# A graph-attention layer: scores by seven block products onto seeded PSUM banks, masks of a whole batch at once, one listed order for all engines of the loop

## The chip, the cores and the metric

The kernel runs on one core of one Trainium2 chip. Five engines of that core work beside each other, each through its own instructions in their written order: PE (TensorE, matrix products into PSUM), DVE (VectorE), ACT (ScalarE), POOL (GpSimd) and SP (SyncE, which here only issues DMAs). They wait for each other through semaphores. The metric is device microseconds of one execution, and lower is better; the time of a kernel is the median of several executions.

## The reference, cut to what matters

`x` is 16 batches x 512 nodes x 512 features. There are 16 heads of 32 features, 20 neighbours (the first 20 nodes of a batch), 11 edge labels and two directions.

```python
self_feat = concat(x, where(x.sum(-1) == 0, 0, q)) @ W_self.T + b_self
output = self_feat
for d in range(2):
    A = (adj if d == 0 else adj.swapaxes(1, 2))[:, :, :20]      # 512 x 20 x 11 labels
    cond, vb = A.sum(-1), A @ w_bias + b_bias
    kv = self_feat[:, :20]
    qh, kh = heads(self_feat @ Wq[d].T + bq[d]), heads(kv @ Wk[d].T + bk[d])
    aff = einsum('bnhd,bmhd->bnhm', qh, kh) / sqrt(32)
    w = softmax(where(cond > 0, aff, -9e15) + vb, axis=-1)      # over the 20 neighbours
    output += per_head_output(einsum('bnhm,bmf->bnhf', w, kv), Wout[d], bout[d])
return x + relu(output)
```

## The kernel before

All is float32, and features lie on the 128 partitions in four chunks (`C`). A set-up stage loads the weights, makes the neighbours' features and keys, and folds `Wq` into the keys: a batch then has a matrix `g` (512 features x 608 columns; 608 is 16 heads x 2 directions x 19, since the scores of neighbour 0 are subtracted from the others). The `g` of batches 2 to 15 are written to DRAM (`g_d`) from staging tiles `st` and read back by the loop. The set-up ends with a run of PE bursts (`keys`, line 696) between which other products are put.

The loop goes over 16 batches, and in a batch over four tiles `nt` of 128 nodes. For each tile:

- PE: `scores` (line 356). Two halves `g` of 64 nodes, four feature chunks `k` and two halves `a` of the heads make 16 matrix products of a 128x64 stationary block with 304 moving columns; a float32 product is two passes, so the trace has 32 instructions for a tile. The two halves `a` go to different halves of the PE's columns and run side by side.
- POOL: `full_add` (line 346) adds key bias and mask of the tile into `full`.
- DVE: `weigh` adds scores and `full` (369), takes the largest of each 20 (373) and subtracts it (377). ACT: `expo` (382). DVE: `normal` sums (415) and inverts (416); POOL multiplies (417). DVE: `turn` transposes the weights into `wt` (406, 408).

Once in a batch: `product` (line 283) makes the features of the *next* batch by seven products of half-size blocks (n = 1 to 7, 16 instructions each) in place of eight, whose terms `partial` (290) and `joined` (300) put together on DVE and whose operands `x_sum` (248) makes on POOL. `mask_mul` (318), `mask_count` (323, 324), `mask_sum` (329) and `mask_spread` (337) make the masks in two halves of 256 nodes. `attend` (435) multiplies the weights `wt` of the batch before with its values `vd` into four PSUM banks; `finish` adds `self_feat` to them on DVE (459), applies the bias and the relu on ACT (463), and `residual` adds `x` on POOL (468).

The order is the order in which the loop's code issues the steps; a planner isn't involved. The last batch has a path of its own: its last tile is worked in two halves, and `self_feat`, bias and `x` are put into the output banks by PE (`put_self`, 803) ahead of `attend`, so that little is left behind the last product.

Of the kernel before, what the change touches and what calls it, by code (L numbers as in the profile page):

```python
# [18 lines left out]
def gat_kernel(  # L19
# [66 lines left out]
    g0 = const.tile([P, C, WD], F32, name="g0")  # L86
# [9 lines left out]
    xs, xns, rss, adjs, nzs, sfs, cqs, gs, vds = {}, {}, {}, {}, {}, {}, {}, {}, {}  # L96
    adds, fulls, wts, outs, held, sf_ps, conds, prods = {}, {}, {}, [], [None] * 3, {}, {}, {}
    sums, parts, us, done = {}, {}, {}, {}


    def behind(one, other):

        if other is not None:
            info = mybir.DependencyInfo(mybir.DependencyClass.Sync, mybir.DependencyReason.DATA)
            tc.add_manual_dep(one.ins, other.ins.name, info, reason="loads in turn")
# [87 lines left out]


    def self_feat(b, f, h, parts=((0, range(C)), (1, range(C)))):


        lo, hi = max(NG, h * N // 2), (h + 1) * N // 2
        for i, ks in parts:
            if (i, ks[0]) == (0, 0):  # L200
                if (f, h) == (0, 0):
                    new_self(b)
                held[0] = bank(f"ps_sf{b}_{f}{h}", 3 if (f, h) == (1, 1) else None)
            for k in ks:
                for a in range(HA):
                    nc.tensor.matmul(  # L206
                        held[0][bass.ts(a, RA), i * N // 2 : i * N // 2 + hi - lo],
                        ws_v[:, k, bass.ds((2 * f + i) * P + a * RA, RA)], xs[b][:, k, lo:hi],
# [5 lines left out]
    def self_copy(b, f, h):  # L214

        lo, hi = max(NG, h * N // 2), (h + 1) * N // 2
        ps = sf_ps.pop((b, f, h))
# [32 lines left out]
    def product(b, n):  # L250
# [11 lines left out]
        if n == 1:  # L262
            parts[b, "a"] = [bank(f"ps_a{b}_{i}", i) for i in range(2)]
        if n == 2:
            parts[b, "d"] = bank(f"ps_d{b}", 2)
        if n == 5:
            parts[b, "c"] = bank(f"ps_c{b}", 3)
# [811 lines left out]
```

## Time and profile before

| what | value |
|---|---|
| median of 3 runs | 587.99 us (587.1 to 588.12) |
| profiled execution | 589.11 us, of which 587.3 us are the span that the profile covers |
| mean granted PE clock | 0.994 |
| busy share of the span | PE 98%, DVE 85%, POOL 65%, ACT 50% |

The profile gives, for each engine, busy time and groups of instructions by line; a timeline gives start and length of each run of equal instructions, and what an engine that stood idle waited for. The times of a PE run include the tail in which its last columns drain, so the distance from one start to the next says what a run costs. In the rows, the part ahead of `<-` is what is written, the part behind it what is read; `x32` is a count.

### The profile page before, as it was taken

The numbers are of one execution on the slowest core, as the hardware profiler recorded it, in microseconds if no ns is written. First come the engines' busy times: TensorE is split into PE (matmuls) and PEld (weight loads), VectorE is DVE, ScalarE is ACT, GpSimd is POOL, SyncE is SP. The second block draws the span as 40 slices with busy tenths as digits, with TensorE's granted clock in tenths as the row PEclk, the third lists the DMA queues.
The fourth block names the chain that finished last, engine by engine and source line by source line (L and its number), as shares of the span: only waits on it lengthen the run. The fifth ranks groups of instructions, "written<-read, shape, count | busy, mean of one in ns | idle before, by whom it ended". The sixth has DMA issues, their size and how long they took to land.

```text
span 587.3 us, 15688 instructions
## 1 busy us (share of the span) xinstructions
PE 578.5 (98%) x6188; PEld 353.2 (60%) x6188; DVE 497.3 (85%) x850; ACT 296.4 (50%) x778; POOL 382.0 (65%) x351
## 2 busy tenths in 40 slices
PE   8999999999999999999999999999999999999995
PEld 5444547886666665656565656565666656666654
DVE  0495565889999999999998989898989899999996
ACT  1234442546464646555564646464747474645441
POOL 2315663658677776858585868685858585867774
PEclk9999999999999999999999999999999999999997
DMA  8999999855858484868586767667665757582513
GB/s 298 382 404 312 349 371 322 243 146 159 232 153 242 150 249 158 246 153 237 150 247 164 215 172 227 173 212 197 177 207 183 222 167 228 159 242 68 169 37 127
DMA packets 93434, 125.56 MB, mean 214 GB/s; under 512 B 11217, under 2 KB 65521, under 8 KB 91313
## 3 DMA queue, kind: packets, MB, share of 16 engines
q1 hardware_dynamic: 92112, 122.67, 68.0%
q0 software_dynamic: 672, 1.36, 1.1%
q8 instruction: 49, 0.80, 0.5%
q10 hardware_dynamic: 576, 0.53, 0.3%
q14 instruction: 25, 0.20, 0.1%
HBM read 85.71 MB, written 39.19 MB: 213 GB/s over the span
## 4 chain that ended last, share of the span: by engine, by line
PE 94%; DVE 3%; DMA 1%; issue 0%; ACT 0%; SPq 0%; POOL 0%; DVEq 0%; POOLq 0%; ACTq 0%
PE ps_s L356 44%; PE ps_a L283 17%; PE ps_c L283 8%; PE ps_o L435 6%; PE ps_d L283 4%; PE ps_v L671 3%; PE ps_k L607 3%; PE ps_sf L206 2%; DMA ws_q<-in_wsT 1%; PE ps_kv L557 1%; DVE o L459 0%; PE ps_nz L190 0%; DVE ps_s L373 0%; DVE full L369 0%; DVE sm L415 0%
## 5 line engine op out<-in xcount | busy, mean ns | idle before, releaser
L356 PE MATMUL ps_s<-g,sf 128*64 128x304 f32 x2048 | 273.6, 420 | 0.5 <-ACT st L711 0.5
L356 PEld LDWEIGHTS ps_s<-g,sf 128*64 128x64 f32 x2048 | 152.1, 137 | 107.5 <-issue 6.2
L417 POOL TENSOR_TENSOR s<-s,sm 128x640 f32<-128x640 f32 x63 | 80.2, 1273 | 130.4 <-DVE sm L416 127.9
L382 ACT ACTIVATE s<-s 128x640 f32<-128x640 f32 x63 | 46.5, 737 | 163.6 <-DVE s L377 163.6
L318 ACT ACTIVATE prod<-adj,wb_sb 128x80 f32<-128x80 int32 x330 | 111.6, 427 | 0.0
L346 POOL TENSOR_TENSOR full<-cq,both 128x640 f32<-128x640 f32 x64 | 99.5, 1555 | 2.7 <-ACT both L337 1.5
L369 DVE TENSOR_TENSOR full<-ps_s,full 128x608 f32<-128x608 f32 x63 | 49.8, 791 | 31.4 <-PE ps_s L356 26.1
L468 POOL TENSOR_TENSOR o<-o,x 128x512 f32<-128x512 f32 x60 | 75.5, 1279 | 0.0
L337 ACT COPY both<-add 64x80 f32<-64x80 f32 x128 | 32.8, 256 | 52.0 <-DVE add L329 50.6
L283 PE MATMUL ps_a<-t,ws_s 128*64 128x246 f32 x480 | 55.1, 371 | 0.0
L373 DVE TENSOR_REDUCE ps_s<-full 128x32 f32<-128x640 f32 x63 | 52.2, 828 | 2.2
L377 DVE TENSOR_TENSOR s<-full,ps_s 128x640 f32<-128x640 f32 x63 | 51.5, 818 | 1.1
L415 DVE TENSOR_REDUCE sm<-s 128x32 f32<-128x640 f32 x63 | 50.8, 806 | 1.6 <-ACT s L382 0.9
L406 DVE STREAM_TRANSPOSE wt<-s 128x512 f32<-128x512 f32 (+1 forms) x65 | 45.3, 696 | 0.1
L283 PEld LDWEIGHTS ps_a<-t,ws_s 128*64 128x64 f32 x480 | 35.5, 137 | 15.9
L435 PE MATMUL ps_o<-wt,vd 32*32 32x256 f32 (+4 forms) x1360 | 42.8, 382 | 1.5 <-DVE wt L408 1.5
L329 DVE TENSOR_REDUCE add<-prod 128x80 f32<-128x960 f32 x32 | 36.8, 1150 | 5.9 <-ACT prod L318 3.9
L463 ACT ACTIVATE o<-o,bo 128x512 f32<-128x512 f32 x60 | 38.2, 710 | 1.2 <-POOL biased L911 1.2
L248 POOL TENSOR_TENSOR t<-x 128x492 f32<-128x492 f32 x30 | 34.4, 1148 | 4.9 <-DVE full L369 4.9
L435 PEld LDWEIGHTS ps_o<-wt,vd 32*32 32x32 f32 (+1 forms) x1360 | 26.2, 122 | 17.6 <-issue 12.2
L459 DVE TENSOR_TENSOR o<-ps_o,sf 128x512 f32<-128x512 f32 x60 | 36.7, 668 | 0.0
L290 DVE SCALAR_TENSOR_TENSOR u<-nz,qw,ps_a 128x246 f32<-128x246 f32 x90 | 36.6, 448 | 0.0
(238 smaller groups left out, 766.6 us busy)
## 6 DMA issues: line engine op xcount, KB each, us to landing
g_d<-st SPq DMA_DIRECT2D x16, 1064.0 KB, 5.7
g<-g_d SPq DMA_DIRECT2D x28, 608.0 KB, 4.9
out_T<-o SPq DMA_DIRECT2D x60, 256.0 KB, 4.5
xn<-in_xn SPq DMA_DIRECT2D x28, 512.0 KB, 3.6
x<-in_xT SPq DMA_DIRECT2D x28, 512.0 KB, 4.4
adj<-in_adj SPq DMA_DIRECT2D x32, 440.0 KB, 4.4
vd<-bd_d SPq DMA_DIRECT2D x64, 64.0 KB, 3.9
nz<-nz_d SPq DMA_DIRECT2D x14, 256.0 KB, 3.4
```

The source lines that it names most:

```text
L283: nc.tensor.matmul(to, lhs, x[:, k], start=start, stop=stop, skip_group_check=n != 2)
L318: nc.scalar.activation(p[:, :, l], a[:, :, l], AF.Identity, scale=wb_sb[:, l : l + 1])
L346: nc.gpsimd.tensor_add(f, cqs[b].unsqueeze(1).to_broadcast(shape), adds[b, nt // 2][:, nt % 2].unsqueeze(2).to_broadcast(shape),)
L356: nc.tensor.matmul(bank[bass.ts(a, RA), :WA], sfs[b][:, k, bass.ds(nt * P + g * RA, RA)], keys[:, k, a], start=(k == 0), stop=(k == C - 1),)
L369: nc.vector.tensor_add(f[:, :, :, 1:], ps[:, :, :WA].rearrange("p g (h m) -> p g h m", m=ND), f[:, :, :, 1:])
L373: nc.vector.tensor_reduce(mx, f, AX.X, ALU.max)
L377: nc.vector.tensor_sub(s, f, mx.unsqueeze(3).to_broadcast(full))
L382: done["exp"] = nc.scalar.activation(sw, sw, AF.Exp)
L415: nc.vector.tensor_reduce(sm, s, AX.X, ALU.add)
L417: done["normal"] = nc.gpsimd.tensor_mul(s, s, sm.unsqueeze(3).to_broadcast(full))
L435: nc.tensor.matmul(banks[q][to, bass.ts(c, w)].rearrange("p (t g n) -> p t g n", g=HA, n=32), lhs, rhs, start=start and first and c == 0, ...
L468: nc.gpsimd.tensor_add(o[:, c], o[:, c], xs[b][:, c])
```

## The change

**Scores.** The nodes of a batch are put in another order (two halves of 256 that each begin with ten of the neighbours), and nodes, features and heads are split so that the score matrix of a batch is a 2x2 by 2x2 block product. It is made by seven block products (`score_product`, P1 to P7) in place of eight: 16 products of 128x64 with 152 moving columns each (4 tiles of 64 nodes, `j`, x 2 feature chunks x 2 halves `a`). Their operands need sums: of blocks of `self_feat` (`self_sum`, S1 to S4) and of blocks of the keys (`key_sum`, T2, T1, T4), all on POOL; one difference of the key weights is taken in the set-up (`weight_differences`).

**Seeds.** The PSUM banks are held for the whole loop: `ps_a`, `ps_w`, `ps_e` (two banks each), `ps_u`, `ps_v` (one each). Products are never started afresh in the first three: ACT writes the starting value (key bias into `ps_a`, masks into `ps_w`, a difference of key biases into `ps_e`, `self_feat` with its bias into the output banks, which are `ps_w` and `ps_e` again), and PE adds. ACT and DVE copy intermediate sums out of `ps_a` (`u1`, `u2p`, `u3p`). The softmax works on four units of 2x64 x 4 tiles (c11, c22, c21, c12), each [128 x 640] as before; mask and bias no longer pass through `full`, and `full_add` and `finish` are gone. The features' seven products go through `ps_u` and `ps_v` with such seeds too.

**Masks** of a batch are made at once: 11 multiplications of 160 rows on ACT in place of 22 of 80, one count and one sum on DVE, and four copies in place of eight.

**Order.** One list gives every step of every engine for a batch, with the distance in batches (`P1:0` this batch, `f1:-1` the next, `OUT:1` the one before, `reluW:2` the one before that). The loop runs it from period -3 to 19 and leaves out what is not there. The last batch has no path of its own any more.

```diff
-    def scores(b, nt, g, bank, ks=range(C)):
-        keys = gs[b].rearrange("p c (a w) -> p c a w", a=HA)
-        for k in ks:
-            for a in range(HA):
-                nc.tensor.matmul(
-                    bank[bass.ts(a, RA), :WA], sfs[b][:, k, bass.ds(nt * P + g * RA, RA)], keys[:, k, a],
-                    start=(k == 0), stop=(k == C - 1),
-                )
+    def score_product(b, n):
+        rows, keys, to = {
+            1: (lambda: self_block(b, 0, 0), lambda: key_block(b, 0), ps_a),
+            2: (lambda: self_block(b, 0, 1), lambda: key_block(b, 1), ps_w),
+            3: (lambda: sums[b, "s", 4], lambda: key_block(b, 2), ps_e),
+            4: (lambda: self_block(b, 1, 1), lambda: sums[b, "t", 4], ps_a),
+            5: (lambda: sums[b, "s", 1], lambda: sums[b, "t", 1], ps_e),
+            6: (lambda: sums[b, "s", 2], lambda: sums[b, "t", 2], ps_a),
+            7: (lambda: sums[b, "s", 3], lambda: key_block(b, 3), ps_a),
+        }[n]
...
+        for k in range(2):
+            for j in range(C):
+                for a in range(HA):
+                    nc.tensor.matmul(
+                        to[bass.ts(a, RA), j, :, 1:], rows[:, k, bass.ts(j, RA)],
+                        keys[:, k, a].rearrange("p (x m) -> p x m", m=ND),
+                        start=False, stop=k == 1, skip_group_check=True,
+                    )
+    def seed_scores(b):
+        nc.scalar.copy(grid(ps_a), over_groups(cqs[b][:, 0]))
+    def first_part(b):
+        us[b, "1"] = score_part(b, 1)
+        nc.scalar.copy(us[b, "1"], grid(ps_a))
+    def masked_part(b, n):
+        us[b, str(n)] = score_part(b, n)
+        nc.vector.tensor_add(by_head(us[b, str(n)]), by_head(grid(ps_a)), mask_of(b, n - 2))
+    def unit(b, i, l):
+        t = soft_w[b, i, l] = soft.tile([P, C, FW], F32, tag=f"s{i}{l}", name=f"s{b}_{i}{l}", bufs=1)
+        if (i, l) == (1, 0):
+            nc.vector.tensor_add(by_head(t), by_head(grid(ps_a)), mask_of(b, 1))
+        else:
+            n, of = {(0, 0): ("1", ps_w), (0, 1): ("2", ps_e), (1, 1): ("3", ps_e)}[i, l]
+            nc.vector.tensor_add(t, grid(of), us.pop((b, n)))
+    def mask_mul(b):
+        for l in range(L):
+            nc.scalar.activation(label_sums(b)[:, :, l], labels(b)[:, :, l], AF.Copy, scale=wb_sb[:, l : l + 1])
+    def seed_out(b, a):
+        for c in range(HA):
+            n = a * HA + c
+            nc.scalar.activation(out_banks(a, c), turned(sfs[b][:, n]), AF.Identity, bias=bo[:, n : n + 1])
+    order = """
+        S3:0 sr21:1 P1:0 Lv:1 reluW:2 S2:0 tr11:1 Lcq:-1 reluE:2 sr12:1 f1:-1 nm21:1 Lt3:-1 u1:0 cnt:-1 seedE:0
...
+        soE:1 sb21:0 ex12:0 nm22:0 OUT:1 ex21:0 j12:-1 cfin:-1 seedA:-1 S1:-1 tr22:0 Lnz:-2
+        clear_blocks(zero)
+        for period in range(-3, B + 4):
+            for name, back in order:
+                b = period - back
+                if 0 <= b < B and (name, b) not in made:
+                    steps[name](b)
+            if period == 0:
+                blocks()
```

What this does to the order is shown at three places, where `x16` counts products (two passes each) and a name's last number tells buffers apart.

PE, one batch in the middle of the loop, before (`ps_s`: scores of a tile; `ps_a`, `ps_c`, `ps_d`: features of the next batch), starting behind `attend`:

```order
L356 MATMUL ps_s_2_2154<-g_1931,sf_1951 64x304 x16
L283 MATMUL ps_a_0_2244<-x_2065,ws_v 64x246 x4
L283 MATMUL ps_a_1_2245<-x_2065,ws_v 64x246 x4
L283 MATMUL ps_d_2254<-x_2065,ws_v 64x246 x8
L283 MATMUL ps_a_0_2244<-t_2_2148,ws_s 64x246 x4
L283 MATMUL ps_a_1_2245<-t_2_2148,ws_s 64x246 x4
L356 MATMUL ps_s_3_2281<-g_1931,sf_1951 64x304 x16
```

The same engine after the change, from behind `attend` on (`ps_a`, `ps_w`, `ps_e`: P1, P6, P2, P5, P7, P4, P3; `ps_u`, `ps_v`: features; two more feature products and `attend` follow):

```order
L413 MATMUL ps_a<-g_1101,sf_2758 64x8x19 x16
L277 MATMUL ps_u<-x_2827,ws_v 64x246 x8
L413 MATMUL ps_a<-k_2_2813,s_2_2958 64x8x19 x16
L413 MATMUL ps_w<-g_1101,sf_2758 64x8x19 x16
L413 MATMUL ps_e<-k_1_2829,s_1_2922 64x8x19 x16
L413 MATMUL ps_a<-g_1101,s_3_2929 64x8x19 x16
L277 MATMUL ps_u<-t_2_3068,ws_s 64x246 x8
L413 MATMUL ps_a<-k_4_2834,sf_2758 64x8x19 x16
L277 MATMUL ps_v<-x_2827,ws_v 64x246 x8
L413 MATMUL ps_e<-g_1101,s_4_3115 64x8x19 x16
L277 MATMUL ps_u<-t_3_3140,ws_s 64x246 x8
L277 MATMUL ps_v<-t_1_3040,ws_s 64x246 x8
```

Four runs of 304-column products have become seven of 152-column ones, and `ps_a` is filled four times in a batch, each time after somebody has read it.

POOL where set-up and loop meet, before (`full`: mask and bias of a tile, `t`: operands of the feature products, `s`: softmax weights):

```order
L720 COPY g_81<-st_1031 128x152
L346 TENSOR_TENSOR full_1_1112<-cq_749,both_0_748 128x640
L248 TENSOR_TENSOR t_1_1114<-x_171 128x492
L417 TENSOR_TENSOR s_0_1107<-s_0_1107,sm_0_1129 128x640
L248 TENSOR_TENSOR t_2_1176<-x_171,t_1_1114 128x492
```

And after (`k`: sums of key blocks T2, T1, T4; `s`: sums of feature blocks S1, S3, S2):

```order
L785 COPY g_79<-st_1033 128x152
L430 TENSOR_TENSOR cqd_1112<-cq_751 128x160
L386 TENSOR_TENSOR k_2_1121<-g_79 128x608
L386 TENSOR_TENSOR k_1_1123<-g_79,k_2_1121 128x608
L386 TENSOR_TENSOR k_4_1125<-g_79,k_2_1121 128x608
L396 TENSOR_TENSOR s_1_1128<-sf_718 128x512
L396 TENSOR_TENSOR s_3_1130<-sf_718 128x512
L396 TENSOR_TENSOR s_2_1148<-s_1_1128,sf_718 128x512
L251 TENSOR_TENSOR t_1_1216<-x_172 128x492
```

Six sums now stand on POOL between the last key block and the second score product, which reads the first and the last of them.

DVE in the second half of a batch, after (`s_10`, `s_01`, `s_11`: softmax units 21, 12, 22; `sf<-ps_v`: features joined):

```order
L447 TENSOR_TENSOR s_10_2054<-ps_a,both_1681 128x640
L307 TENSOR_TENSOR sf_2006<-ps_v,f_1_1877 128x2x246
L460 TENSOR_REDUCE ps_a<-s_10_2054 128x32
L450 TENSOR_TENSOR s_01_2079<-ps_e,u_2_1914 128x640
L460 TENSOR_REDUCE ps_a<-s_11_2008 128x32
L460 TENSOR_REDUCE ps_e<-s_01_2079 128x32
L464 TENSOR_TENSOR s_11_2008<-s_11_2008,ps_a 128x640
L307 TENSOR_TENSOR sf_2006<-ps_v,f_3_2093 128x2x246
L464 TENSOR_TENSOR s_01_2079<-s_01_2079,ps_e 128x640
```

Before, add, maximum and difference of one tile stood behind each other there:

```order
L369 TENSOR_TENSOR full_1_2107<-ps_s_1_2111,full_1_2107 128x32x19
L373 TENSOR_REDUCE ps_s_1_2111<-full_1_2107 128x32
L377 TENSOR_TENSOR s_1_2142<-full_1_2107,ps_s_1_2111 128x640
L406 STREAM_TRANSPOSE wt_2145<-s_0_2100 128x512
L408 STREAM_TRANSPOSE wt_2145<-s_0_2100 128x128
```

Now three units are taken in turn, and the difference of unit 12 (the last row above) releases the ACT seed of `ps_e` that `attend` adds to.

More of the change, by code (lines that the diff above doesn't have):

```diff
@@ L94, in gat_kernel @@
     nz_d = dram.tile([B, N], F32, name="nz_d")
[L96 to L105, printed above, removed]
@@ L261, in product @@
         x = x()
[L262 to L267, printed above, removed]
+        to = ps_v if n in (2, 3, 5) else ps_u
         for i in range(2):
@@ new lines, in feature_seed, with feature_join, label_sums @@
+    def feature_seed(b, f):
+        for i in range(2):
+            nc.scalar.activation(
+                ps_v[:, bass.ts(i, HN)], nzs[b][:, half(f)], AF.Copy, scale=qw[:, 2 * f + i, b : b + 1]
+            )
+    def feature_join(b, f, l, n):
+        nc.vector.tensor_add(sfs[b][:, 2 * f : 2 * f + 2, half(l)], side(ps_v), us.pop((b, n)))
+    def label_sums(b):
+        if b not in prods:
+            prods[b] = msk.tile([P, C * S, L + 1], F32, tag="prod", name=f"prod{b}", bufs=1)
+        return prods[b]
@@ L335, in mask_spread, with mask_sum @@
+    def mask_sum(b, rows=slice(0, C * S)):
+        if rows.start == 0:
+            sums[b, "mask"] = msk.tile([P, C * S], F32, tag="add", name=f"add{b}", bufs=1)
+        nc.vector.tensor_reduce(sums[b, "mask"][:, rows], prods[b][:, rows], AX.X, ALU.add)
+    def mask_spread(b, units=(0, 1), halves=range(HA)):
+        at = slice(units[0], units[-1] + 1)
+        if b not in both:
+            both[b] = msk.tile([P, 2, C, S], F32, tag="both", name=f"both{b}")
         for a in halves:
             for g in range(HA):
-                nc.scalar.copy(
-                    adds[b, h][bass.ts(a, RA), :, g], add[bass.ts(g, RA)].rearrange("p (t m) -> p t m", t=2)
-                )
@@ L426, in attend @@
-    def attend(b, banks, tiles=slice(0, NT), start=True, stop=True):
-        n = tiles.stop - tiles.start
-        w = n * HA * 32
-        heads = wts[b][:, tiles, : W * 4 // 5].rearrange("p t (g j n) -> p t g j n", g=HA, n=32)
-        ends = wts[b][:, tiles, W * 4 // 5 :].rearrange("p t (g j n) -> p t g j n", g=HA, n=32)
-        def mm(q, c, to, lhs, rhs, first):
+                to = both[b].rearrange("p i (y x) m -> p i y x m", x=HA)[bass.ts(a, RA), at, :, g]
+                of = sums[b, "mask"].rearrange("p (i y m) -> p i y m", i=2, m=S)[bass.ts(g, RA), at]
@@ L437, in mm @@
-                start=start and first and c == 0, stop=stop and not first, skip_group_check=True,
+                (ps_w, ps_e)[a][to, g, bass.ts(c, NH)].rearrange("p (i j n) -> p i j n", i=2, n=32), lhs, rhs,
+                start=False, stop=True, skip_group_check=True,
             )
@@ L685, in gat_kernel, with weight_differences @@
             HB = B // 2
+            def weight_differences(hg):
+                low, high = (wq_sb[:, :, hg, bass.ts(j, HF)] for j in range(2))
+                nc.gpsimd.tensor_sub(low, high, low)
             def keys(runs):
@@ new lines, in gat_kernel @@
+    made = {
[3 rows of a table added]
+    }
+    made = {(name, b) for b, names in made.items() for name in names.split()}
+    order = """
+        S3:0 sr21:1 P1:0 Lv:1 reluW:2 S2:0 tr11:1 Lcq:-1 reluE:2 sr12:1 f1:-1 nm21:1 Lt3:-1 u1:0 cnt:-1 seedE:0
+        Lk21:-1 res3:2 seedD:0 P6:0 cu1:-1 Lk22:-1 nm12:1 lab:-1 tr21:1 St3:2 P2:0 xs1:-1 u2p:0 Lk11:-1 tr12:1
+        cqd:-1 res1:2 P5:0 c11:0 xs2:-1 St1:2 mx11:0 sb11:0 res0:2 P7:0 ex11:0 xs4:-1 Ladj1:-2 sd:-1 f6:-1 u3p:0
+        msc:-1 rs34:-2 St0:2 sr11:0 S4:0 P4:0 Ladj2:-2 nself:-1 c22:0 rs12:-2 xs3:-1 u2s:-1 nm11:0 soW:1 lsum:-1
+        f2:-1 Lxn1:-3 fl:-2 res2:2 P3:0 Snz:-2 Lxn2:-3 c21:0 spread:-1 T2:-1 j11:-1 mx21:0 sc:-1 f7:-1 Lx2:-2
+        T1:-1 c12:0 mx22:0 T4:-1 f5:-1 mx12:0 cu3:-1 St2:2 sb22:0 Lx1:-2 f4:-1 ex22:0 j22:-1 sb12:0 sr22:0 f3:-1
+        soE:1 sb21:0 ex12:0 nm22:0 OUT:1 ex21:0 j12:-1 cfin:-1 seedA:-1 S1:-1 tr22:0 Lnz:-2
```

705 lines of the change are left out of this document (276 added, 429 removed), and 3 rows, old and new, of the table made.

## The prediction, on record before the run

> **What bounds the kernel now.** I read the page's totals and its chain first:
>
> ```profile
> span 587.3 us, 15688 instructions
> PE 578.5 (98%) x6188; PEld 353.2 (60%) x6188; DVE 497.3 (85%) x850; ACT 296.4 (50%) x778; POOL 382.0 (65%) x351
> PE 94%; DVE 3%; DMA 1%; issue 0%; ACT 0%; SPq 0%; POOL 0%; DVEq 0%; POOLq 0%; ACTq 0%
> ```
>
> PE is the bound: it is never idle, and the chain that ended last is PE for 94%. Next the timeline of PE over one batch, and busy times of all engines in that stretch:
>
> ```profile
> 305.79 4.26 PE L356 MATMUL ps_s<-g,sf 128*64 128x304 f32 x32
> 309.88 1.83 PE L283 MATMUL ps_c<-x,ws_s 128*64 128x246 f32 x16
> 311.54 4.26 PE L356 MATMUL ps_s<-g,sf 128*64 128x304 f32 x32
> 315.73 2.57 PE L435 MATMUL ps_o<-wt,vd 32*128 32x256 f32 x80
> 318.23 4.32 PE L356 MATMUL ps_s<-g,sf 128*64 128x304 f32 x32
> 322.38 1.83 PE L283 MATMUL ps_a<-x,ws_v 128*64 128x246 f32 x16
> ...
> 336.45 1.45 PE L356 MATMUL ps_s<-g,sf 128*64 128x304 f32 x10
> ```
> ```profile
> 305.79:336.45 30.66, 30.66 (x323) 18.65 (x321) 28.25 (x48) 17.30 (x48) 21.88 (x19) 1.00 0.71 198
> ```
>
> By the starts: scores of a tile 4.09 us, a feature product 1.66, attend 2.50; 4 x 4.09 + 7 x 1.66 + 2.50 = 30.48, and the batch lasts 30.66. So 0.18 is stall and the rest is columns. The second row gives PE, PEld (weight loads), DVE, ACT, POOL: 30.66, 18.65, 28.25, 17.30, 21.88.
>
> **Scores.** 4.09 us for 32 instructions of 304 columns, two side by side, is 0.256 per pair, 0.84 ns a column. Seven products of 16 pairs and 152 columns are 112 x 0.128 = 14.32 us, if nothing but columns counts; now 16.36. The nearest rows for short runs are these (a set-up burst, whose four row groups run side by side; then weight loads; then the narrowest products):
>
> ```profile
> 70.73 0.29 PE L696 MATMUL ps_g(2, 2, 1, 0, 2)0_846<-khD,wq_sb 32*128 32x152 f32 x2
> 70.86 0.29 PE L696 MATMUL ps_g(2, 2, 1, 0, 2)0_846<-khD,wq_sb 32*128 32x152 f32 x2
> L356 PEld LDWEIGHTS ps_s<-g,sf 128*64 128x64 f32 x2048 | 152.1, 137 | 107.5 <-issue 6.2 <-ACT st L711 0.7
> L803 PE MATMUL ps_o<-biased,ident 128*128 128x64 f32 x16 | 2.0, 279 | 0.0
> ```
>
> 152 columns follow each other after 0.13 us there, though each needs a new load of 128 columns. A 64-column load takes 137 ns, but two run side by side (152.1 / 2048 = 74 ns each). The narrowest, with 128-column loads, still cost 125 ns each (2.0 / 16). Bounds for a pair: 0.128 (columns alone) and 0.149 (two loads of 74 ns in turn). I take 0.128, by the 152-column rows. Features and attend keep their sizes: PE per batch 14.32 + 11.62 + 2.50 = 28.44; with a stall as now, 28.6.
>
> [...]
>
> **The other engines must fit into 28.6.**
>
> ```profile
> L369 DVE TENSOR_TENSOR full<-ps_s,full 128x608 f32<-128x608 f32 x63 | 49.8, 791 | 31.4 <-PE ps_s L356 26.1 <-issue 3.1 <-POOL t L248 2.2
> L373 DVE TENSOR_REDUCE ps_s<-full 128x32 f32<-128x640 f32 x63 | 52.2, 828 | 2.2
> L415 DVE TENSOR_REDUCE sm<-s 128x32 f32<-128x640 f32 x63 | 50.8, 806 | 1.6 <-ACT s L382 0.9
> L459 DVE TENSOR_TENSOR o<-ps_o,sf 128x512 f32<-128x512 f32 x60 | 36.7, 668 | 0.0
> L329 DVE TENSOR_REDUCE add<-prod 128x80 f32<-128x960 f32 x32 | 36.8, 1150 | 5.9 <-ACT prod L318 3.9 <-POOL prod L324 2.0
> L290 DVE SCALAR_TENSOR_TENSOR u<-nz,qw,ps_a 128x246 f32<-128x246 f32 x90 | 36.6, 448 | 0.0
> L300 DVE TENSOR_TENSOR sf<-ps_c,u 128x492 f32<-128x492 f32 x30 | 19.3, 645 | 0.0
> L318 ACT ACTIVATE prod<-adj,wb_sb 128x80 f32<-128x80 int32 x330 | 111.6, 427 | 0.0
> L382 ACT ACTIVATE s<-s 128x640 f32<-128x640 f32 x63 | 46.5, 737 | 163.6 <-DVE s L377 163.6
> L463 ACT ACTIVATE o<-o,bo 128x512 f32<-128x512 f32 x60 | 38.2, 710 | 1.2 <-POOL biased L911 1.2
> L417 POOL TENSOR_TENSOR s<-s,sm 128x640 f32<-128x640 f32 x63 | 80.2, 1273 | 130.4 <-DVE sm L416 127.9
> L346 POOL TENSOR_TENSOR full<-cq,both 128x640 f32<-128x640 f32 x64 | 99.5, 1555 | 2.7 <-ACT both L337 1.5
> L468 POOL TENSOR_TENSOR o<-o,x 128x512 f32<-128x512 f32 x60 | 75.5, 1279 | 0.0
> ```
>
> DVE loses `finish` (4 x 0.67) and gains two 640-wide adds (`u2p`, `u3p`, 2 x 0.82, scaled from 608); one count and one sum of twice the length save about 0.3: 28.25 - 2.67 + 1.64 - 0.3 = 26.9. It stays 1.7 under PE.
>
> ACT gains `u1` and three seeds (4 x 0.74), four output seeds (4 x 0.71), two feature copies (2 x 0.6, between 320 and 512 wide) and four half-width seeds (4 x 0.45): 8.8. The 22 label multiplications become 11: now 111.6 / 15 = 7.4 us a batch, then between 11 x 0.43 = 4.7 (width free) and again 7.4 (width is all). 17.3 + 8.8 - 2.7 to 0 is 23.4 to 26.1.
>
> POOL loses four `full_add` (6.2) and gains four S (1.28 each), three T (608 wide, between 1.28 and 1.56, taken 1.42) and one short difference (0.5): 21.9 - 6.2 + 5.1 + 4.3 + 0.5 = 25.6.
>
> So all three fit by sums. SP's queue carries the same bytes (198 GB/s in the row above) in another order: value loads and `Lcq` first, then the keys between the stores, then adjacency, `xn` and `x`. The adjacency now has one buffer: its load waits for the multiplications and the count of the batch before, and has most of a period to land. `Lx2` waits for the last residual add of two batches ago, and behind it stand the other half, a store and the flags; the first reader comes some 12 us later. I cost this at nothing; the cover is that distance, and if it goes, xs1 and f1 are late. The set-up's two weight differences (POOL, 1.28 each) lie beside the key products and cost nothing either.
>
> Waits in the steady loop. DVE instructions that don't wait for each other overlap a little:
>
> ```profile
> 569.62 0.82 DVE L377 TENSOR_TENSOR s<-full,ps_s 128x640 f32<-128x640 f32 x1
> 570.36 0.70 DVE L406 STREAM_TRANSPOSE wt<-s 128x512 f32<-128x512 f32 x1
> ```
>
> The 0.82 us one hands over after 0.74, so 0.08 is saved. The tightest chain begins behind P7: on DVE `u3p`, c22, c21, c12 and the differences sb22, sb12 (6 x 0.82), a sum with its inversion (0.81 + 0.35), two feature terms (0.90), the mask sum (2 x 1.15 less one fixed part, 2.15), two joins (1.30) and three maxima (2.49): 12.9, less 14 x 0.08 is 11.8, and 0.2 for PE's tail. ACT then writes two output seeds (1.42) before `attend` may add to `ps_e`: 13.4. PE spends from P7's end six feature products and P4, P3: 6 x 1.66 + 2 x 2.05 = 14.06. Slack 0.6. `u3p` (1.1 with both hand-overs) lies under the feature product ahead of P4 (1.66), `u1` under f1, the sums S1, S3, S2 (3.8) under attend, P1 and f1 (6.2). `seedA` comes behind sb21 on DVE and an exponential on ACT, at 15.6 from P7's end, and P1 is due at 16.6. Had one of these covers gone, PE would wait for that difference in every period. I see none that has, but four within about a microsecond.
>
> **The start.** Rows of PE's and SP's timelines, and the DMA issue:
>
> ```profile
> 91.09 0.29 PE L696 MATMUL s_g(3, 3, 1, 1, 2)0_1046<-khD,wq_sb 32*128 32x152 f32 x2
> 96.06 3.69 PE L206 MATMUL ps_sf<-x,ws_v 128*64 128x256 f32 x32
> 121.76 1.52 PE L356 MATMUL ps_s<-g,sf 128*64 128x304 f32 x10
> 92.29 0.32 SPq L722 DMA_DIRECT2D g_d<-st  x1
> g_d<-st SPq DMA_DIRECT2D x1, 1064.0 KB, 4.6
> 105.14 1.65 SPq L159 DMA_DIRECT2D bd_d<-vw_d  x2
> 118.92 1.75 SPq L142 DMA_DIRECT2D vd<-bd_d  x4
> ```
>
> Batch 1's scores now begin at 121.76. After the change the last burst (row 91.09, until 91.3) is followed by the last features of batch 0 (2 x 1.66, now inside the first batch at 96.06), their way out of PSUM (1.0), zeroing of the banks (1.9, seven 512-wide products on four row groups) and `seedA` (0.75): P1 starts at 98.4, and with one feature product PE is busy to 102.1. P6 needs T2 and S2. T2's memory was a staging tile that goes to DRAM until 92.29 + 4.6 = 96.9; behind that stand T2, T1, T4, S1, S3, S2 on POOL, 3 x 1.42 + 3 x 1.28 = 8.1: P6 at 105.1, a stall of 3.0. From P6 to the next batch's P1 are three more products to P7's end (8.2), and from there DVE's chain to sb21 and `seedA` (15.3): batch 1 begins at 128.6.
>
> In its period the queue of SP holds the value loads behind the ten DMAs of `blocks`, which took 105 to 118.9; the loads behind them (`Lcq`) free POOL's `cqd` late, and with it xs2 and f6. I estimate 2 us on PE (0 to 4). Batch 1 then counts from 130.6: 8.9 later than now.
>
> **The end.**
>
> ```profile
> 551.05 4.26 PE L356 MATMUL ps_s<-g,sf 128*64 128x304 f32 x32
> 582.91 0.28 DVE L1011 TENSOR_TENSOR o<-ps_o,x 128x128 f32<-128x128 f32 x1
> ```
>
> The last batch takes 587.33 - 551.05 = 36.3 us now, 4.1 of it behind the last instruction. After: P1 to P3 with two waits of 1.1 (for `u1` and `u3p`, no feature product hides them) 16.5; c12, two maxima, four differences and sums and a transposition on DVE to the sum of unit 21 and then 12, 27.0; a multiplication (1.27), an add of batch 14 (1.28) and another multiplication on POOL, partly beside that, 29.4; transposition 30.3; attend 33.0; four relus (0.55 each) 35.2; four adds of `x` 40.2; DMA and close 4.3: 44.5, or 8.2 more.
>
> **Sum.** Fourteen batches lie between: 14 x (30.66 - 28.6) = 28.8 saved, 8.9 and 8.2 given back: 587.3 - 11.7 = 575.6 us of span. The profiled execution took 589.1, 1.1 above the median; I take the difference off the median 587.99: 576.
>
> **Rivals.**
> *DVE's chain sets the period.* If its 14 steps take their whole durations, the chain of 13.4 is 14.5, and with a hand-over of 0.06 at half a dozen semaphores 14.9: 0.85 over PE's 14.06, so a period of 29.4 and 576 + 15 x 0.8 = 588. For it: DVE is 26.9 of 28.6 full, and it waits for PE three times a period, which a sum of busy times doesn't see. Against: DVE is now at 28.25 of 30.66 and PE loses 0.18. It decides the sign at a period of 29.4.
> *Loads set the pace of PE* (the slower side). 224 loads x 74 ns = 16.6 us of scores, as many as now: the period is 30.9, start and end are still paid: 576 + 15 x 2.3 = 610. Slower from 0.138 a pair on. Against: the 152-column rows.
> *Start and end cost less.* If T2's memory is free at once and SP's queue isn't felt, 5 us; the period at 28.45 gives 2 more: 569.
> *No change of PE work* can't be: the columns are fewer by an eighth.
>
> **Chances.** As summed, 570 to 582: 0.62. DVE's chain or a like wait in each period: 0.22, over 582 to 598 (0.10 of it faster, 0.05 level, 0.07 slower). Cheap ends, 567 to 570: 0.11. Loads: 0.05. The range 567 to 588 leaves out the loads and the longer half of the waits. Within 0.2% of 588 (586.8 to 589.2, about what a measurement of this kernel can tell from no change) 0.05; faster 0.62 + 0.11 + 0.10 = 0.83; slower 0.12.
>
> **What would show it.** Score products of 32 instructions about 2.05 us apart (right) or over 2.2 (loads). A period of 28.4 to 28.8. PE idle before P6 of batch 0 for some 3 us, released by POOL `s2`; another gap in batch 1 behind `cqd`. From the last batch's P1 to the end some 44 us. PE waiting in every period for ACT's output seed or `seedA` would make the forecast wrong.

## The result, and the profile after

The changed kernel takes 583.44 us in the median of four runs (582.67 to 584.66), the kernel before 587.81 beside it: a ratio of 0.9929 (95% interval 0.9908 to 0.9951), 4.4 us less. The forecast was 576.0, 12 less. The profiled execution after took 582.67, 0.8 under its median, that of before 589.11, 1.3 above the median of these runs; so the two profiles differ by 6.4 in span, 2.1 more than the medians.

The page's totals after, and its row of granted clock:

```profile
span 580.9 us, 18537 instructions
PE 551.2 (95%) x7626; PEld 423.7 (73%) x7626; DVE 453.1 (78%) x718; ACT 370.6 (64%) x768; POOL 443.6 (76%) x399
PEclk9999999899999999999999999999999999999965
```

PE is still the bound, but its share fell from 98% to 95%: it now waits at the start and at the end. The last digits of the clock row (6, 5) are new as well: the granted clock was 0.50 from 554 to 560 and from 566 to 580. The busy times from batch 1's P1 to batch 15's P1, and PE's timeline in a steady batch:

```profile
131.80:534.70 402.90, 402.74 (x5825) 334.58 (x5825) 357.30 (x550) 303.63 (x632) 353.94 (x305) 1.00 0.68 198
```
```profile
247.19 2.29 PE L413 MATMUL ps_a<-g,sf 128*64 128x152 f32 x32
249.30 1.83 PE L277 MATMUL ps_u<-x,ws_v 128*64 128x246 f32 x16
250.96 2.24 PE L413 MATMUL ps_a<-k,s 128*64 128x152 f32 x32
253.03 2.24 PE L413 MATMUL ps_w<-g,sf 128*64 128x152 f32 x32
...
271.68 1.83 PE L277 MATMUL ps_v<-x,ws_s 128*64 128x246 f32 x16
273.44 0.48 PE L505 MATMUL ps_w<-wt,vd 32*128 32x256 f32 x2
...
275.94 2.29 PE L413 MATMUL ps_a<-g,sf 128*64 128x152 f32 x32
```

Fourteen batches take 402.90, PE idle for 0.16 of it. A score product takes 2.07 from start to start (P1, behind `attend`, 2.11), and every batch from 2 on lasts 28.75. Per batch DVE has 25.5, ACT 21.7, POOL 25.3. The loop gained what its columns promised, nearly; what came back is at the two ends. The start on PE, POOL's first sum, and the granted clock there (the third number from the end of a row):

```profile
99.42 2.29 PE L413 MATMUL ps_a<-g,sf 128*64 128x152 f32 x32 [0.79 <-ACT ps_a L420]
101.54 1.83 PE L277 MATMUL ps_u<-x,ws_v 128*64 128x246 f32 x16
106.13 3.65 PE L413 MATMUL ps_a<-k,s 128*64 128x152 f32 x32 [2.76 <-POOL s L396]
109.57 2.59 PE L413 MATMUL ps_w<-g,sf 128*64 128x152 f32 x32
111.99 2.24 PE L413 MATMUL ps_e<-k,s 128*64 128x152 f32 x32
```
```profile
97.93 1.46 POOL L386 TENSOR_TENSOR k<-g 128x608 f32<-128x608 f32 x1 [5.88 <-DMA g_d<-st]
```
```profile
106.00:108.00 2.00, 1.87 (x20) 1.81 (x22) 0.31 (x1) 2.00 (x5) 1.28 (x2) 0.72 1.06 350
108.00:110.00 2.00, 2.00 (x19) 1.89 (x18) 0.12 (x1) 1.56 (x4) 0.82 (x2) 0.50 1.16 320
```

P6 waits 2.76 for S2, as forecast; but then it takes 3.44 to P2's start and P2 2.42, at clocks of 0.72 and 0.50. Batch 1 begins at 131.80, 10.0 later than before. The end: PE ahead of attend of batch 14, POOL, and the chain of the page's fourth part in its last 19 us (start, length, engine, what):

```profile
557.02 0.79 PE L505 MATMUL ps_e<-wt,vd 32*128 32x256 f32 x2 [4.71 <-ACT ps_e L496]
```
```profile
560.42 1.27 POOL L477 TENSOR_TENSOR s<-s,sm 128x640 f32<-128x640 f32 x1 [2.20 <-DVE sm L473]
563.55 1.27 POOL L527 TENSOR_TENSOR o<-o,x 128x512 f32<-128x512 f32 x1 [1.86 <-ACT o L523]
564.77 1.28 POOL L477 TENSOR_TENSOR s<-s,sm 128x640 f32<-128x640 f32 x1
```
```profile
561.85 1.57 ACT o L523 x3
563.42 0.59 ACT ps_w L496
...
565.37 0.70 ACT ps_e L496
...
566.11 1.22 PE ps_e L505 x4
...
571.86 0.60 ACT o L523
...
573.08 1.26 POOL o L527
574.34 1.22 POOLq L983
575.56 2.44 POOL o L527 x2
```

PE waits 4.7 for the output seed of batch 14 and then runs attend at half clock (0.50 from 556 to 560). Relus of batch 14 (L523) and output seeds of batch 15 (L496) stand on ACT one behind the other, and attend of batch 15 waits for the last of them; on POOL the multiplication nm12 (564.77) stands behind an add of batch 14, which waited 1.86 for those relus. Four adds of 1.23 end it. From P1 of batch 15 to the end are 580.9 - 534.7 = 46.2, before 36.25.

| part of the span | forecast | profile |
|---|---|---|
| 14 batches | 14 x 2.06 = -28.8 | 402.9 - 0.38 - 429.29 = -26.8 |
| start, with batch 1's stall | +8.9 | 131.80 + 0.38 - 121.76 = +10.4 |
| end | +8.2 | 46.2 - 36.25 = +9.95 |
| sum | -11.7 | -6.4 |

### The profile page after: what moved, and what is told of

Its sections match the earlier page's. It is cut to its first block, busy times and chain, and to the rows that moved or that the text cites. A ratio compares the mean times of both kernels' runs of the same rounds, so it can differ in the third digit from the quotient of the medians.

```text
span 580.9 us, 18537 instructions
## 1 busy us (share of the span) xinstructions
PE 551.2 (95%) x7626; PEld 423.7 (73%) x7626; DVE 453.1 (78%) x718; ACT 370.6 (64%) x768; POOL 443.6 (76%) x399
## 4 chain that ended last, share of the span: by engine, by line
PE 78%; POOL 2%; SPq 2%; DMA 2%; ACT 1%; DVE 1%; issue 1%; POOLq 0%; ACTq 0%
PE ps_a L413 22%; PE ps_u L277 16%; PE ps_v L277 12%; PE ps_e L413 11%; PE ps_w L505 6%; PE ps_w L413 5%; PE ps_e L505 2%; PE ps_v L730 2%; PE ps_sf L205 1%; SPq L160 1%; POOL k L386 1%; DMA g_d<-st 1%; SPq L156 1%; POOL s L396 1%; POOL o L527 1%
## 5 line engine op out<-in xcount | busy, mean ns | idle before, releaser
L334 ACT ACTIVATE prod<-adj,wb_sb 128x160 f32<-128x160 int32 x165 | 80.4, 588 | 0.0
L441 DVE TENSOR_TENSOR u<-ps_a,both 128x640 f32<-128x640 f32 x32 | 26.4, 824 | 38.1 <-PE ps_a L413 34.6
L277 PE MATMUL ps_u<-t,ws_s 128*64 128x246 f32 x480 | 55.0, 371 | 0.2 <-POOL t L251 0.2
L505 PE MATMUL ps_e<-wt,vd 32*32 32x256 f32 (+1 forms) x640 | 44.4, 418 | 4.8 <-ACT ps_e L496 4.7
L386 POOL TENSOR_TENSOR k<-g,k 128x608 f32<-128x608 f32 x32 | 46.9, 1486 | 1.3
L505 PE MATMUL ps_w<-wt,vd 32*32 32x256 f32 (+1 forms) x640 | 44.3, 416 | 3.6 <-ACT ps_w L496 3.6
L483 DVE STREAM_TRANSPOSE wt<-s 128x512 f32<-128x512 f32 x64 | 44.1, 689 | 4.6 <-POOL s L477 4.6
L396 POOL TENSOR_TENSOR s<-sf 128x512 f32<-128x512 f32 x32 | 40.3, 1281 | 1.0
L413 PE MATMUL ps_a<-k,s 128*64 128x152 f32 x512 | 37.2, 300 | 3.7 <-POOL s L396 2.8
L413 PE MATMUL ps_a<-g,sf 128*64 128x152 f32 x512 | 36.6, 296 | 2.2 <-ACT ps_a L420 2.2
L339 DVE TENSOR_REDUCE cond<-adj 128x160 f32<-128x1760 int32 (+1 forms) x17 | 31.1, 1830 | 7.8 <-DMA adj<-in_adj 7.8
L413 PE MATMUL ps_a<-k,sf 128*64 128x152 f32 x512 | 35.8, 293 | 0.9 <-DVE u L441 0.9
```

The source lines that it names most:

```text
L277: nc.tensor.matmul(to[bass.ts(a, RA), bass.ts(i, HN)], lhs, x[:, k], start=(n, i, k) == (1, 0, 0), stop=k == 1, skip_group_check=True,)
L334: nc.scalar.activation(label_sums(b)[:, :, l], labels(b)[:, :, l], AF.Copy, scale=wb_sb[:, l : l + 1])
L386: op(t, one(), two())
L396: op(t, one(), two())
L413: nc.tensor.matmul(to[bass.ts(a, RA), j, :, 1:], rows[:, k, bass.ts(j, RA)], keys[:, k, a].rearrange("p (x m) -> p x m", m=ND), start=Fals ...
L483: nc.vector.transpose(wts[b][:, i, l, : W * 4 // 5], t[:, :, :MW])
```

## The experiments

Each experiment starts from the changed kernel unless it says otherwise. The first number is its median time; behind it stand the ratio to the kernel before, timed beside it, and the 95% interval of that ratio. e8 and e12 have one execution each.

**e1_warm: half clock as a cost.**
```diff
+def warm(n): n x matmul(ps_v[:, :96], zero, zero[:, :96], start=False)
+ # 20 ahead of P6:0, 34 and 36 ahead of the last two OUT:1
```


> Products of zeros (128 by 128 weights, 96 columns, added to ps_v) are put into PE's three long waits: 20 ahead of P6 of batch 0, 34 ahead of attend of batch 14, 36 ahead of attend of batch 15. Nothing else waits for less. Theory A (PE's clock falls to half when PE has waited, and that makes start and end longer than their waits): the granted clock stays at 1.00, P6 and P2 of batch 0 take 2.07 us each instead of 3.44 and 2.42, attend of batch 14 some 2.5 instead of 4.3, attend of batch 15 some 2.6 instead of 3.6: 1.7 + 1.8 + 1.0 = 4.5 us less, 579 us. Rival B (start and end are long by their waits alone, and the clock follows rather than causes): the products run, the rest stays where it is, 583.4. Rival C (idle PE is not what lowers the clock): the clock falls all the same, 583.4 or more.

585.85, 0.9974 (0.9955 to 0.9994): 2.4 slower than the changed kernel. The clock stayed (mean 0.99; P6 2.12, P2 2.07, attends 2.57 each), so it was PE's rest that had lowered it. But twenty of these products last longer than the wait:

```profile
103.78 4.71 PE L871 MATMUL ps_v<-zero 128*128 128x96 f32 x40
```

P6 starts 4.63 behind the first of them, so one takes 0.23 us, and the waits were overfilled: behind its batch's P1, P6 came 1.8 later than in the changed kernel, attend of batch 14 2.4. Batch 1 besides lost 4.0: f6 waited 2.11 there, and behind that wait the clock fell to 0.50 all the same (windows from 147 to 150). What the clock costs stayed open.

**e2_start: POOL's order for batch 0.**
```diff
-T2:-1 T1:-1 T4:-1 S1:-1 | S3:0 S2:0
+T2:-1 S1:-1 | S2:0 T1:0 S3:0 T4:0
```


> Only POOL's order for batch 0 is changed: T2, S1, S2, then T1, S3, T4, where it was T2, T1, T4, S1, S3, S2. The first sum still waits for the staging tile's way to DRAM. Theory A: S2 is ready some 4 us behind T2's begin at 97.9, ahead of f1's end, so P6 follows f1 at once at 103.4 (2.8 earlier), and without that wait the clock does not fall (another 1.7): 4.5 us less, 579. Rival B (the clock's fall has another cause than the wait): 2.8 less, 580.6. Rival C (batch 1 begins late for another reason, its keys or cq by DMA): P6 comes earlier but P1 of batch 1 stays at 131.8, 583.4.

581.54, 0.9872 (0.9845 to 0.9899). P6 follows f1 without a wait and at full clock (2.07 to P2's start), and batch 1's P1 comes 27.73 behind that of batch 0 instead of 32.38. Yet batch 1 now lasts 32.87 instead of 29.13: of 4.7 us, 3.7 are gone by batch 2. POOL and PE in batch 1:

```profile
139.56 0.52 POOL L430 TENSOR_TENSOR cqd<-cq 128x160 f32<-128x160 f32 x1 [5.93 <-DMA cq<-cq_d]
```
```profile
141.23 1.05 PE L277 MATMUL ps_u<-t,ws_s 128*64 128x246 f32 x6 [2.22 <-POOL t L251]
```

Rival C, almost: f6 waits for xs2, behind `cqd`, behind the load of cq, and just behind its begin at 141.23 the clock falls (0.93 in the window from 140 to 142, 0.50 from 142 to 144), which adds to the loss. The changed kernel has the same wait on POOL, 3.86 in its profile, of which 0.38 reached PE.

**e3_end: order at the end.**
```diff
-res3:2 nm12:1  (period 16)
+nm12:1 ... res3:2
-reluW reluE res3 res1 res0 res2 (POOL), batch 15
+reluW add0 add1 reluE add2 add3 (DVE)
```


> Only the order at the end is changed: the last residual add of batch 14 stands behind the multiplication nm12 of batch 15 on POOL, and the four adds of x of batch 15 go to DVE, each behind its two halves of relu, where POOL made them behind all relus. Theory A (the end is long by its order of steps): nm12 comes 2.7 earlier, attend of batch 15 then waits for ACT's output seed (566.06) and begins 1.0 earlier; the last add ends 0.7 behind the last relu instead of 5.0: 5.4 us less, 578. Rival B (the last stores set the end, 1 MB at some 200 to 250 GB/s is 4 to 5 us from the first add on): 2 to 3 us less, 581. Rival C (the end hangs on nothing but DVE and PE): 0 to 1 less.

578.65, 0.9846 (0.982 to 0.9871). From the last P1 to the end 42.1 instead of 46.2. All of it is the adds at the end. On POOL nm12 now stands ahead of the add of batch 14, and DVE's last transposition is done at 566.35, 29.75 behind P1 (32.3 in the changed kernel); yet attend of batch 15 did not begin earlier. DVE's row, and the chain:

```profile
566.08 0.27 DVE L484 STREAM_TRANSPOSE wt<-s 128x128 f32<-128x128 f32 x1
```
```profile
567.38 0.70 ACT ps_e L496
568.08 0.04 issue
568.12 0.80 PE ps_e L505 x2
```

It waits for ACT's output seed, and that stands behind the relus of batch 14. I had it 1.0 earlier.

**e4_all: e2, e3 and the zeros at the end.**

> The orders of e2 and e3 together, and the 34 and 36 products of zeros ahead of the last two attends. Theory A: the gains add up, 4.5 at the start, 5.4 at the end, and the clock at the end another 2 to 2.8: 571. Rival B (waits alone): 2.8 + 5.4 = 8.2 less, 575. Rival C (the loop takes back what the start gains, because batch 1 waits for its loads): 577 or more.

577.7, 0.9829 (0.9804 to 0.9854). Not additive, and by its time rival C. Batch 1 lost 2.5 to the same wait, and the zeros (34 and 36) were again too many: the end is 44.1, worse than e3's 42.1.

**e5_blocks: SP's order in period 0.** In the changed kernel SP and POOL run like this when batch 1 begins:

```profile
123.50 3.88 SPq L156 DMA_DIRECT2D bd_d<-vw_d  x2
127.42 7.79 SPq L160 DMA_DIRECT2D bd_d<-vw_d  x8
...
139.12 1.14 SPq L125 DMA_DIRECT2D cq<-cq_d  x2
```
```profile
142.50 0.53 POOL L430 TENSOR_TENSOR cqd<-cq 128x160 f32<-128x160 f32 x1 [3.86 <-DMA cq<-cq_d]
```
```diff
-            if period == 0: blocks()          # at the period's end
+todo.insert(todo.index(("Lk11", -1)) + 1, ("blocks", 0))
```


> Only SP's order in period 0 is changed: the ten DMAs of the value blocks stand behind the key loads of batch 1, where SP had nothing to do from 106 to 117, instead of at the period's end, ahead of the value loads of batch 0 and of cq of batch 2. Batch 1's scores have taken 0.4, 4.0, 4.1, 2.4 and 2.5 us more than a steady batch in the five profiles so far, each time ahead of f6, which waits for x_sum xs2, which stands on POOL behind the difference cqd. Theory A (cq comes late because SP's queue is full of the blocks): batch 1 takes 28.75 like the others, 0.4 to 4 us less than in the kernel after the change, 579 to 583, and the runs scatter less. Rival B (cq is late because its own transfer is slow, or another load holds xs2): batch 1 still loses 0.4 to 4, no gain.

580.15, 0.9862 (0.9838 to 0.9886), 3.3 us under the changed kernel. Batch 1 lasts 28.75, and `cqd` waits for nothing:

```profile
136.25 0.52 POOL L430 TENSOR_TENSOR cqd<-cq 128x160 f32<-128x160 f32 x1
```

Theory A: the queue of SP was the reason for batch 1's stall. What the stall costs is not separated by the 3.3, though. The two profiles differ by 2.9 in span; 0.4 of that is batch 1, and 1.7 is P6 and P2 of batch 0, which ran at full clock in e5 (P6 2.12) behind the same wait (2.74).

**e6_warm: e5 with 11, 21 and 20 zeros.**

> As the kernel with the moved blocks, and products of zeros in PE's three long waits, now counted by the 0.23 us that one took before (20 took 4.7 us, longer than the wait): 11 ahead of P6 of batch 0, 21 and 20 ahead of the last two attends. Theory A (half clock after a wait costs time at both ends): 1.7 at the start and about 1.8 + 1.9 at the end less than the kernel with the moved blocks alone, together about 5 us. Rival B (what PE loses there lies beside DVE's and ACT's work): 1.7 or less. Rival C: the products themselves delay by some 0.2 each place, so 0.

578.94, 0.9837 (0.9811 to 0.9862): 1.2 under e5, with intervals that overlap, so unclear by time, and no more than rival B's 1.7. In the profiles the start is the same (in e5's the clock had not fallen: P6 2.12), and attend of batch 15 ends 2.9 earlier behind its P1 (32.8 against 35.7). The kernel's end comes only 1.5 earlier, and ACT's row says why:

```profile
565.99 1.09 ACT L523 ACTIVATE o<-ps_w 128x512 f32<-128x512 f32 x2 [4.63 <-DMA out_T<-o]
```

The relus wait for the tile `o`, whose stores of batch 14 are still under way: the next wait behind the one removed.

**e7_ends: both ends together.**
```diff
+ # batch 15's output in ps_u, ps_v and ps_a; its seeds ahead of the relus of 14
-ps_u, ps_v = two tiles
+ps_uv = one tile of two banks; ps_u, ps_v = its halves
+ # period 16: soW soE sr12 sr21 nm12 nm21 tr22 tr12 tr21 | reluW:2 reluE:2 res:2 ... OUT
```


> All that the runs so far point to: the moved blocks, POOL's order of T2, S1, S2 at the start, and at the end the output seeds of batch 15 in other banks (ps_u, ps_v and ps_a, free by then) so that they need not wait for the relus of batch 14; the last sums, multiplications and transpositions ahead of anything of batch 14; the adds of x on DVE; products of zeros ahead of the last two attends. Theory A (start and end are long by waits that order alone makes): the start 4.5 shorter, batch 1 without a stall, attend of batch 15 begins when DVE's last transposition allows, about 28.2 behind its P1 instead of 31.4, takes 2.3 instead of 4.5, and 6 us behind it the kernel ends: end 37 instead of 46.2; together 568 to 571. Rival B (the orders gain only what the earlier runs of the ends gave, 2 and 5): 575. Rival C (stores of 1 MB set the end): 572 to 574.

619.64, 1.0526 (1.05 to 1.0551). Attend of batch 15 ends 31.1 behind P1, but the relus behind it wait for the stores of batch 14, as in e6, so that the end is 41.0 and not 37; and each of the steady batches lasts 31.81. From the list of waits (total us, times, longest):

```profile
PE ps_uv L277 <- DVE sf L307: 12.7, 15, 0.8
PE ps_uv L277 <- ACT f L284: 10.7, 15, 0.7
```

None of these waits is in the changed kernel. As halves of one tile the two banks wait for each other's readers. A fault of the edit, but it shows what a merged buffer costs: 3.06 us a batch.

**e8_dve: the slack of DVE's chain.**
```diff
-mx22:0 T4:-1 f5:-1 mx12:0
+mx22:0 mx22:0 T4:-1 f5:-1 mx12:0 mx12:0
```


> Two of DVE's maxima (mx22 and mx12) are made twice in every period: 2 x 0.74 us more in the chain from P7 to the output seed ahead of attend, and 1.5 more in DVE's busy time (25.5 of 28.75 before). The results are the same. Theory A (PE's columns set the period, with the forecast slack of 0.6 in that chain): the period grows by 0.9, to 29.6, with a wait of PE ahead of attend for ACT's seed. Rival B (DVE's chain sets the period already): it grows by 1.5, to 30.2. Rival C (the slack is larger than was worked out): 28.8 to 29.2.

One run, 598.39; the period is 29.75, 1.00 more. Of 1.48 added, 0.48 was free: theory A by the period, with 0.5 for the 0.6 worked out. The wait is not where it was expected. PE loses 0.6 ahead of f3, whose bank DVE's join (line 307) has yet to read, and only 0.35 in attend:

```profile
305.94 1.88 PE L277 MATMUL ps_v<-x,ws_s 128*64 128x246 f32 x16 [0.42 <-DVE sf L307]
```

So the change has brought DVE's chain to within half a microsecond of PE.

**e9_all: e7 mended.**
```diff
+ # ps_u, ps_v two tiles again; batch 15's o in the free wt buffer; add2, add3 of 14 on DVE
+ # zeros: 19 and 12
```


> The orders of e7_ends again, with ps_u and ps_v as separate tiles (one tile for both had made features wait for each other's bank in every batch), the output of batch 15 in memory of its own instead of the tile whose stores of batch 14 are still on their way, half of batch 14's adds on DVE, and 19 and 12 products of zeros. Theory A: the loop is back at 28.75; the start is 2.9 shorter than with the moved blocks alone; attend of batch 15 ends 31.1 behind its P1 (35.7 there), then relus 2.2, the last add 0.7 and 2.9 to the end: 36.9 instead of 46.0. 580.15 - 2.9 - 9.1 = 568. Rival B (stores: 2 MB of two batches in 6 us): 571 to 573. Rival C (orders at the ends give no more than e2_start and e3_end gave): 574 to 576.

570.51, 0.9705 (0.9691 to 0.9719): 2.9% under the kernel before, 12.9 us under the changed one, and between theory A and rival B. The loop is at 28.75 from batch 2 on (batch 1 takes 29.13); P1 of batch 15 to the end 38.1 instead of 46.2. Its chain from 12.6 us before the end on:

```profile
554.97 2.92 PE ps_v L895 x24
557.89 0.41 PE ps_u L516
...
560.83 0.10 ACT o_last L543
...
561.50 0.59 DVE o_last L891
562.11 1.29 DVE o_last L891 x2
```

PE's zeros, attend, relu and DVE's adds follow each other with no wait for batch 14. The zeros now stand in the chain themselves; whether fewer would do was not tried.

**e10_cold: e9 without the zeros.**

> The same without the products of zeros. Theory A (PE at half clock behind a wait costs what the attend takes longer): attend of batch 15 takes 4.5 instead of 2.3 to 2.6, and nothing lies beside it: 2 us more than the kernel with them. Rival B (the clock at the end costs nothing, as the other engines set it): the same time within 0.5. Rival C (products of zeros cost more than they give): less time without them.

572.87, 0.9738 (0.9717 to 0.9758): 2.4 more, with intervals that just touch. In the profile attend of batch 14 takes 4.4 instead of 2.6 from its second group on, at a clock of 0.50, that of batch 15 4.7 instead of 2.7, and the end 41.7 instead of 38.1. The list of waits has PE here behind a load that begins when attend of batch 14 is through:

```profile
PE ps_u L516 <- DMA vd<-bd_d: 2.3, 1, 2.3
```

The two profiles differ by 4.7 and the medians by 2.4: in e10's profile batch 1 also took 0.8 more, since its f1 waited 0.94 for the load of `x`. Theory A all the same: the end alone is 3.6 longer, and half clock lies on its path.

**e11_start: e5 with e2's order.**

> The moved blocks and POOL's order T2, S1, S2 at the start, nothing at the end. Theory A (batch 1's stall had eaten what e2_start gained): P1 of batch 1 comes 27.7 behind P1 of batch 0 (30.7 to 32.4 before) and batch 1 takes 28.75, so 2.9 to 4.6 us less than the moved blocks alone: 575.5 to 577.3. Rival B (batch 1 then meets the next late load and stalls again): 579 to 580.

577.79, 0.9829 (0.9814 to 0.9844): 2.4 under e5, half a microsecond short of the wait of 2.9, with intervals that overlap slightly. Batch 1 comes 27.72 behind batch 0 and lasts 28.92. What e2 gained and lost again is kept once the queue is clear. Rival B is not quite gone: e9 and e10 have the same start, and there f1 of batch 1 waits 0.16 and 0.94 for the load of `x`.

**e12_split: the price of weight loads.**
```diff
-for a in range(HA): matmul(to[.., j, :, 1:], ..)            # P2: 32 x 152 columns
+for part in (0:4, 4:8): for a in ..: matmul(to[.., j, part, 1:], ..)   # 64 x 76
```


> Of the seven score products only P2 is made by 64 instructions of 76 columns instead of 32 of 152: as many columns, twice the weight loads. Theory A (columns alone set PE's pace down to here): P2 stays at 2.07 and the period at 28.75. Theory B (below some width the loads set the pace, 74 ns each as two side by side show): P2 takes 64 x 74 ns = 4.7, the period 31.4, and then 152 columns at 64.6 ns per instruction stand just above the loads' own pace. Between them: a load every 50 ns or so gives 3.2 and 29.9.

One run, 582.4. P2 takes 2.11 instead of 2.07, the period 28.79. PE's timeline has a P2 of a steady batch, and the groups by line and form have its loads:

```profile
252.21 2.28 PE L414 MATMUL ps_w<-g,sf 128*64 128x76 f32 x64
```
```profile
L414 PEld LDWEIGHTS ps_w<-g,sf 128*64 128x64 f32 x1024 | 36.0, 137 | 0.0
```

Here 64 products and as many loads go by in 2.11, 33 ns each, and loads show 36.0 / 1024 = 35. The 74 ns that I had read from before was the time for which loads were under way, shared among them, while a product took 128 ns; it is not a floor. Loads don't bound these products at 152 columns, nor at 76.

## Why the prediction was right and wrong

*The period: right in kind, 0.15 off.* PE's columns carry it. Two terms were mis-sized: seven score products take 14.52 a batch for the 14.32 forecast (2.07 each, 2.11 for P1), and seven feature products 11.73 for 11.62 (1.66 each, but 1.76 for the one ahead of attend). The third was read wrongly: the 0.18 called stall is not idle time, since the same row has PE busy for 30.66 of 30.66, and the steady loop after the change has no stall. 0.20 + 0.11 - 0.16 is the 0.15, or 2.1 in fourteen batches.

*The other engines: they fit, as forecast.* DVE 25.5 for 26.9, POOL 25.3 for 25.6. ACT has 21.7, below the 23.4 to 26.1: the label multiplication (80.4 us in fifteen batches, 5.4 each) lies inside its bracket of 4.7 to 7.4, but four mask copies in place of eight (1.3 for 2.05 a batch) and shorter relus (2.2 for 2.5) were not counted. The slack of 0.6 is 0.5 by e8. So the rival in which DVE's chain sets the period is refuted, and so is the one in which loads do, by e12 (its turning point, 0.138 a pair, should have been 0.135: a period of 29.4 is 0.8 more for 112 pairs). An instruction with its load took 64.6 ns at 152 columns and 33 at 76.

*The start: too cheap.* Forecast 8.9, and 10.4 in the profile. The path was as told (staging tile, six sums, P6, then DVE's chain), the wait of P6 2.76 for 3.0. What was off: the staging tile was free 1.0 later (T2 began at 97.93 for 96.9), so P6 began 1.0 later; half clock behind the wait, which the sum doesn't have, cost 1.7 in this profile; DVE's chain to batch 1 took 0.5 more; and the stall of batch 1, estimated at 2 (0 to 4), was 0.38. In six other kernels with the same queue of SP that stall was 1.7 to 4.1. Why that load lands so differently from run to run was not tried.

*The end: too cheap.* 46.2 for 44.5. DVE's steps ran as listed, sum 12 done at 562.1 for 561.7. The step that failed is the next one, from the last transposition (forecast 30.3 behind P1) straight to attend of batch 15. The sum left out ACT's output seeds of batch 15: they go into the banks that the relus of batch 14 read, so they stand behind those relus, and these behind an attend of batch 14 that had itself waited 4.7 for its seed and then run at half clock. The seeds were done at 566.07, 31.4 behind P1, and attend then took 4.5 at half clock (0.50 from 566 to 572) where I had 2.7: it ended at 35.9 for 33.0. The add of batch 14 on POOL was mis-sized too (nm12 ended at 566.05 instead of 564.1, as the add waited for the same relus), but that held nothing: e3 takes it away, and attend begins as late as before. With the seeds in other banks and the clock kept up, attend ends at 31.1 (e7, mean clock 0.996) and 31.4 (e9, 0.998). The end stood 3.1 late at the last add, and a close of 2.9 instead of 4.3 gave 1.4 back.

*What the misses share.* Both ends were summed from durations of the steady loop, as if PE kept its clock and the neighbouring batch's steps only cost their own time. Of the 7.4 between 576.0 and 583.44, loop, start and end make 2.1, 1.5 and 1.75; the remaining 2.1 is the scatter of the two profiled executions against their medians. No profile of a slower execution was taken, so where those 2.1 lie stays open; batch 1's stall, 0.38 in the profiled execution, is one candidate. No one term fails alone: the loop's gain of 26.8 is nearly the 28.8 forecast, but it is a difference against 20.4 given back, and small errors of one sign in all three halved what was left. Much of the 20.4 is order and not the change's nature: with blocks, sums, adds and banks put right and PE kept at work, e9 has 12.9 of it back. The kernel before was not given the same treatment at its ends, so how much of e9's lead over it is the change's own is not shown.

## What to carry to other kernels

A change that deepens a pipeline pays in the loop and is charged at both ends; read the ends as programs of their own, queue by queue, with the neighbouring batch's steps in them. A wait that is removed uncovers the next late one (here a load behind ten small DMAs, then an output tile still being stored), so a fix that gains little alone may gain in company: e2's start lost most of its gain again, and with the queue clear (e11) it kept it. Where PE has to rest for several microseconds close to the end, look at the granted clock before costing the work behind it: here it was 0.50 behind 4.7 us of rest.

## What the runs showed of the hardware

After PE's rest ahead of attend of batch 14 (4.7 idle in the changed kernel, 4.7 to 6.4 in the others without zeros there) the granted clock was 0.50 to 0.56 in all eight profiles, and attend took 4.0 to 4.4 us from its second group on, against 2.6 in e9 (mean clock 0.998). After a rest of 2.7 to 2.8 at the start it fell in the changed kernel and in e3 (P6 3.44 and 3.60) and not in e5 and e12 (2.12); after one of 2.1 to 2.2 in batch 1, in e1 and e2 and not in e3 and e4 (1.00 until 147 in both). In the changed kernel at the end, and at the start behind P6's wait:

```profile
558.00:560.00 2.00, 2.00 (x41) 0.90 (x36) 1.71 (x4) 0.26 (x1) 0.22 (x1) 0.50 0.00 0
106.00:106.50 0.50, 0.37 (x6) 0.37 (x8) 0.31 (x1) 0.50 (x2) 0.50 (x2) 1.00 1.01 414
110.50:111.00 0.50, 0.50 (x12) 0.50 (x10) 0.20 (x1) 0.00 (x0) 0.42 (x2) 1.00 1.47 336
```

P6 began at 106.13 at full clock; the clock fell between 106.5 and 107, when PE was at work again, and was back at 1.00 by 110.5. By the shares of the windows at its two edges half clock lasted 3.4 us here, and as long in batch 1 of e2 (0.93, 0.50 and 0.71 in the three windows of 2 us from 140 to 146); in e3, where P6 and P2 took 1.7 more than at full clock, an estimated 3.4. So the same rest lowered the clock in one run and not in another, and in two runs one of 2.1 to 2.2 us was enough. With products of zeros in PE's rests the mean clock was 0.991 in e1 and 0.998 in e9, against 0.977 in the changed kernel; one of 128 by 128 weights and 96 columns took 0.23 us (20 in 4.63 in e1).
